# Moving sets of exps from ScalarE to VectorE in three of four head groups, and spreading the adjacency pieces over eight groups

## The chip, the cores and the metric

The kernel runs on one core of a Trainium2 chip. The metric is the time of one execution on the device in microseconds (us). The core has five engines that run side by side, each working through its own instructions in order: TensorE (PE, matrix multiplication into the accumulator memory PSUM), ScalarE (ACT, exponentials and other functions), VectorE (DVE, elementwise work and reductions), GpSimd (POOL) and SyncE (SP), which here only issues DMA transfers. GpSimd issues transfers too. PSUM has eight banks of 512 float32 values in each of its 128 partitions.

## The reference

Four graph layers are applied one after the other to x (3327 tokens, 128 features), each inside a residual sum and a layer normalisation. Almost all the time goes to the first one, an attention in which each of the 128 features acts as a head and the heads' vectors have eight elements:

```python
scale = d ** (-0.5)
q = (x @ Wq.T).reshape(d, n, h)          # d = 128, n = 3327, h = 8
k = (x @ Wk.T).reshape(d, n, h)
v = (x @ Wv.T).reshape(d, n, h)
a = jnp.einsum('dnh,dmh->dnm', q, k) * scale
a = a + spatial_encoding + edge_encoding   # both are adj
a = jax.nn.softmax(a, axis=2)
out = jnp.einsum('dnm,dmh->dnh', a, v)
return out.reshape(n, h * d) @ Wo.T
```

So 128 x 3327 x 3327 exponentials are computed in float32. The other three layers multiply the adjacency matrix (3327 x 3327), normalised by its row or column sums, with x times small weights.

## The kernel before, in words

A first stage computes q, k and v and writes them to memory. Then `attention` runs. It cuts the queries into seven ranges of 476 columns (`CW`) and the keys into 26 tiles of 128, in four key ranges of 7, 7, 6 and 6 tiles (`KBS`). A pair of query range and key range is a block; there are 28, in order of query range and then key range, so that two blocks of seven tiles alternate with two of six. In each block the 128 heads are walked through one by one. Four heads make a group, so a block has 32 groups and the attention has 896. The running number of a group is called n.

**Scores.** The scores of one block stay in seven PSUM banks, `sc`, one per key tile. At a block's first head the transposed adjacency values are written there (L596). After that each head adds only its difference: the operands `kt` and `qt` hold the present head's k and q and, negated, those of the head before (the matmul of L603). Each float32 operand is split into a rounded high part and a low part, which is why 64 rows are contracted. The seven banks are used as three sets, `SETS`: three, two and two tiles in a block of seven, two, two and two in a block of six. Each set has a single buffer. The next head's matmul on a set must wait until the exp of the set is through.

**Exps.** `exponents` takes the sets one after the other, and ScalarE turns each into the numbers `e` with one instruction (L611). In groups whose running number is even, one set, the last of the group's first head, goes to VectorE instead (`vector_exp`, L561 to L574): nine instructions that clamp and scale (L567), round to an integer (L568), take the fraction (L569), build the power of two with a shift (L570), and evaluate a polynomial (L573, five times). L567 reads the scores and so frees the set; the other eight work in SBUF on the single buffers `ey` and `et`.

**Weighing.** `weigh` multiplies the exps of one key tile with the values of the four heads of a group (L628, four matmuls side by side in groups of 32 columns, each with two passes) into the last PSUM bank, `o`. It does so one group later, and three groups accumulate in `o` before VectorE adds it to `acc` (`flush`, L639 and L641). `PLACES` says after which of the twelve sets of the present group each tile of the group before is weighed.

**Order of the work.** All compute engines follow the order in which the instructions are written, and the loop at the end of `attention` writes them. VectorE's steps are kept in a list, `vec`, and let out by two counters in `clock`: one counts the time of the sets, the other the assumed cost of VectorE's steps (`vector_work`). Steps are let out at once where the order demands it: query copies at the start of the next group, an exp before its tiles are weighed. `copy_queries` (L493 to L495) negates and doubles the query rows of the next group after they have arrived. `load_heads` issues the transfers of q and k two groups ahead, `load_values` those of v one group ahead, with a copy on GpSimd (L509).

**Adjacency pieces.** The later layers need the transposed adjacency matrix, its row sums and its column sums. While the attention runs, 91 pieces of 512 x 256 are handled, one in each eight groups (`PACE`). A piece is loaded at n % 8 = 0, transposed and searched for its maximum at 3 (L199, L204), summed by rows and by columns at 5 (L206, L213), and stored by GpSimd at 6 (L234).

Of the kernel before, what the change touches and what calls it, by code (L numbers as in the profile page):

```python
# [20 lines left out]
GROUP = 4  # L21
# [3 lines left out]
PACE = 8  # L25
# [25 lines left out]
def kernel(ctx: ExitStack, tc: tile.TileContext, x, adj, wq, wk, wv, wo,  # L51
# [27 lines left out]
    NHG = D // GROUP  # L79
    KBS = [(0, 7), (7, 7), (14, 6), (20, 6)]  # L80
    assert KBS[-1][0] + KBS[-1][1] == T

    def tokens(t):
        return P - 1 if t == T - 1 else P
# [9 lines left out]
    def flat_ap(dram, at, pattern):  # L94

        f = dram.rearrange("r c -> (r c)")
        if isinstance(at, int):
            base = f[at:at + 1]
        else:
            base = f[ds(at, 1)]  # L100
        return bass.AP(base.tensor, base.offset, pattern)
# [115 lines left out]
    def store_tops(pool, u, top, n):  # L217

        hi = pool.tile([P, 4], F32R, name="rhi")
        nc.vector.tensor_copy(hi, top)  # L220
        lo = pool.tile([P, 4], F32R, name="rlo")
        nc.vector.tensor_tensor(lo, top, hi.bitcast(F32), ALU.subtract)
        for row, sb in enumerate((hi, lo)):
            for i in range(P // n):
                nc.gpsimd.dma_start(out=flat_ap(lead_s[u], row * SUPER + i * P, [[1, n], [n, 4]]),
                                    in_=sb[n * i:n * i + n, :].bitcast(F32))

    def piece_store(pool, u, c, at):
        ns = PIECE // P
        for i in range(4):  # L230
            t = 4 * u + i
            if t < T:
                for q in range(4):
                    nc.gpsimd.dma_start(  # L234
                        out=flat_ap(adjT_s, (t * P + 32 * q) * NP + c * PIECE, [[NP, 32], [P, ns], [1, P]]),
                        in_=at[32 * i:32 * i + 32].rearrange("a (s q) t b -> a q s (t b)", q=4)[:, q])
        if c == NPC - 1:
            nc.vector.tensor_reduce(rsum[:, u, :], sums[u], AX.X, ALU.add)
            if u:
                top = pool.tile([P, 4], F32, name="rtop")  # L240
                nc.vector.tensor_reduce(top, maxima[u], AX.X, ALU.max)
                store_tops(pool, u, top, 32)


    with tc.tile_pool(name="pw", bufs=1) as pw, tc.tile_pool(name="pa", bufs=2) as pa, \
# [110 lines left out]
        d = 0  # L356
# [52 lines left out]
    def attention():  # L409
        with tc.tile_pool(name="acc", bufs=1) as accp, tc.tile_pool(name="kq", bufs=3) as kq, \  # L410
# [14 lines left out]
            blocks = [(min(c, N - CW), kb) for c in range(0, N, CW) for kb in range(len(KBS))]  # L425
            groups = [(b, g) for b in range(len(blocks)) for g in range(NHG)]
            steps = [(b, d) for b in range(len(blocks)) for d in range(D)]

            def load_edges(b):
# [4 lines left out]
                if w < nt * P:  # L434
# [8 lines left out]

            SETS = {7: [(0, 3), (3, 2), (5, 2)], 6: [(0, 2), (2, 2), (4, 2)]}


            PLACES = {7: ((0, 2, 4, 4, 7, 7, 9), (0, 0, 4, 7, 7, 9, 10)),
                      6: ((0, 2, 4, 5, 7, 9), (0, 0, 3, 6, 8, 10))}

            def load_heads(b, g):  # L450

# [45 lines left out]
            def tile_at(nt, i):  # L497

                return (i % 2, i // 2, (i // 2) + ((nt + 1) // 2 if i % 2 else 0))
# [18 lines left out]
            loaded, worked, turning = [], [], []  # L518

            def background(n):  # L520
                if n % PACE == 0 and pieces:
                    u, c = pieces.pop(0)
                    loaded.append((u, c, piece_load(pe, u, c)))
                if n % PACE == 6 and worked:
                    piece_store(pe, *worked.pop(0))

            def background_work(n):
                if n % PACE == 3 and loaded:
                    u, c, ai = loaded.pop(0)
                    steps = piece_work(pe, u, c, ai)  # L530
                    worked.append((u, c, next(steps)))
                    next(steps)
                    clock[1] += 2.4
                    turning.append(steps)
                if n % PACE == 5 and turning:
                    clock[1] += 2.4
                    for _ in turning.pop():
                        pass

            def prepare(b, d):  # L540

                n = b * NHG + d // GROUP
                if d % GROUP == 0:
                    while any(of is None for _, of, _ in vec):
                        vec.pop(0)[2]()
                    if n + 2 < len(groups):
                        heads[groups[n + 2]] = load_heads(*groups[n + 2])
                    if n + 1 < len(groups):
                        values[groups[n + 1]] = load_values(*groups[n + 1])
                    while stores:  # L550
                        store(*stores.pop(0))
                    background(n)

                if d % GROUP == n % 2 and n + 1 < len(groups):
                    vec.extend(copy_queries(*groups[n + 1]))
                if d % GROUP == 3:
                    background_work(n)
# [29 lines left out]
            def exponents(b, d, si):  # L587
                kb = blocks[b][1]
                nt = KBS[kb][1]
                t0, n = SETS[nt][si]  # L590
                s = sc[si]
                if d == 0:
                    for i in range(n):
                        tl = tile_at(nt, t0 + i)[2]
                        for j, (q0, w) in enumerate(subs):
                            nc.tensor.matmul(s[:, i, q0:q0 + w], lhsT=edges[b][0:w, j, tl * P:(tl + 1) * P],  # L596
                                             rhs=ident[0:w, 0:w], is_transpose=True,
                                             start=(j == 0), stop=True, skip_group_check=True)
                kt, qt = heads[b, d // GROUP]
                k = d % GROUP  # L600
                for i in range(n):
                    rg, pos, _ = tile_at(nt, t0 + i)
                    nc.tensor.matmul(s[:, i, 0:CW], lhsT=kt[64 * rg:64 * rg + 64, k, pos * P:(pos + 1) * P],  # L603
                                     rhs=qt[64 * rg:64 * rg + 64, k, :],
                                     start=False, stop=True, skip_group_check=True)
                e = ex.tile([P, (3, 2, 2)[si], CW], F32, tag=f"e{si}", name=f"e{si}", bufs=(6, 7, 8)[si])
                if (b * NHG + d // GROUP) % 2 == 0 and (d % GROUP, si) == (0, 2):
                    vector_exp(e[:, 0:n, :], s[:, 0:n, 0:CW], (b, d // GROUP))
                    clock[1] += 1.2
                else:  # L610
                    nc.scalar.activation(e[:, 0:n, :], s[:, 0:n, 0:CW], AF.Exp, scale=2.0)  # L611
                for i in range(n):
                    es[b, d, t0 + i] = e[:, i, :]
                if d == 0 and si == len(SETS[nt]) - 1 and b + 1 < len(blocks):
                    edges[b + 1] = load_edges(b + 1)
# [38 lines left out]
            queue, place = [], 0  # L654
            with tc.manual_schedule(engines={mybir.EngineType.PE, mybir.EngineType.Activation,
                                             mybir.EngineType.Pool, mybir.EngineType.DVE}):
                edges[0] = load_edges(0)
                for n in range(2):
                    heads[groups[n]] = load_heads(*groups[n])
                for _, _, step in copy_queries(*groups[0]):  # L660
                    step()
                values[groups[0]] = load_values(*groups[0])
                for b, d in steps:
                    prepare(b, d)
                    for si in range(len(SETS[KBS[blocks[b][1]][1]])):
                        vector_work(b)
                        exponents(b, d, si)
                        for _ in range(PLACES[len(queue_of)][d // GROUP % 2 == 0].count(place) if queue else 0):
                            weigh(*queue.pop(0))
                        place += 1  # L670
                    if d % GROUP == GROUP - 1:
                        while queue:
                            weigh(*queue.pop(0))
                        queue_of = [(b, d // GROUP, r) for r in range(KBS[blocks[b][1]][1])]
                        queue, place = list(queue_of), 0
                while queue:
                    weigh(*queue.pop(0))
                while stores:
                    store(*stores.pop(0))
# [283 lines left out]


    attention()
    wide = nc.values_load(flag[0:1, 0:1], min_val=0, max_val=1)
    with tc.If(wide > 0):
# [162 lines left out]
    with tc.manual_schedule(engines={mybir.EngineType.PE, mybir.EngineType.SP}):  # L1130
# [18 lines left out]
        for t in range(T):  # L1149
            n = tokens(t)  # L1150
# [15 lines left out]
        for t in range(T):  # L1166
            n = tokens(t)
# [15 lines left out]
        for t in range(T):  # L1183
            n = tokens(t)
# [16 lines left out]
        for t in range(T):  # L1201
            n = tokens(t)
# [35 lines left out]
```

## Time and profile before

| | us |
|---|---|
| median of 3 runs | 10949.95 |
| lowest and highest run | 10942.28, 10952.19 |
| profiled execution, its own time | 10954.31 |
| profiled execution, first to last instruction (span) | 10952.1 |
| busy: TensorE matmul, ScalarE, VectorE | 10557.4, 9867.2, 7291.7 |
| exps on ScalarE, two tiles: 8512 at | 0.999 |
| exps on ScalarE, three tiles: 1792 at | 1.390 |
| first step of exps on VectorE, two tiles: 448 at | 1.150 |

The profile shows one execution. "Busy" is the time in which an engine has at least one instruction under way. Neighbouring instructions overlap on TensorE and on ScalarE, so that the mean of one times their number is more than the busy time. In group rows a bar separates the number of instructions, the busy time and the mean, and after a second bar comes the idle time of the engine ahead of these instructions with what ended it. A tile name such as `sc` or `e` stands for all of its buffers.

### The profile page before, as it was taken

To read this page: it belongs to the slowest core of one execution; us is meant where nothing else is said; L and a number is where in the kernel's file an instruction comes from. 1 tells how busy PE (TensorE), PEld (TensorE's weight loads), DVE (VectorE), ACT (ScalarE), POOL (GpSimd) and SP (SyncE) were. 2 spreads that over 40 slices of the span, in tenths; PEclk is the share of its full clock that TensorE was granted. 3 is DMA by queue.
4 is the path that set the end of the run, shared out by engine and by line. 5 is a ranking of instruction groups with operands and counts; after the bars stand their busy time and mean duration, and the time that the engine had idled before them with its cause. 6 is when DMAs were issued, how large, how long until landed. Compare 5 with 4: busy or idle time off the path is not lost. (4 is left out here: it accounts for less than half of the span.)

```text
span 10952.1 us, 201583 instructions
## 1 busy us (share of the span) xinstructions
PE 10557.4 (96%) x76941; PEld 4117.7 (38%) x76941; DVE 7291.7 (67%) x8351; ACT 9867.2 (90%) x10783; POOL 1585.4 (14%) x2742
## 2 busy tenths in 40 slices
PE   8899999999999999999999999999999999999999
PEld 5333333333333333333333333333333333333779
DVE  6566776667776677766777667776677766667412
ACT  3799999999999999999999999999999999999400
POOL 0111122111221111211112111121111100001200
PEclk9899999999999999999999999999999999999999
DMA  7988888888888888888888888888888888888676
GB/s 251 155 127 122 128 133 132 127 123 129 134 132 128 123 127 132 135 123 127 128 132 134 120 122 120 123 132 125 127 127 123 120 119 116 115 112 117 207 284 244
DMA packets 995053, 1516.11 MB, mean 138 GB/s; under 512 B 202471, under 2 KB 812577, under 8 KB 980267
## 3 DMA queue, kind: packets, MB, share of 16 engines
q1 hardware_dynamic: 896854, 1371.75, 78.7%
q0 software_dynamic: 79616, 116.88, 4.6%
q8 instruction: 623, 10.21, 0.5%
q10 hardware_dynamic: 17620, 14.49, 0.4%
q14 instruction: 340, 2.79, 0.1%
HBM read 1371.86 MB, written 130.35 MB: 137 GB/s over the span
## 5 line engine op out<-in xcount | busy, mean ns | idle before, releaser
L611 ACT ACTIVATE e<-sc 128x952 f32<-128x952 f32 (+1 forms) x10304 | 9644.5, 1067 | 227.8 <-PE sc L603 219.9
L628 PE MATMUL o<-e,v_pad 128*32 128x476 f32 (+1 forms) x46592 | 5639.9, 573 | 39.9 <-DVE acc L641 36.7
L603 PE MATMUL sc<-qt,kt 64*128 64x476 f32 x23296 | 4474.9, 438 | 252.6 <-ACT e L611 167.3
L603 PEld LDWEIGHTS sc<-qt,kt 64*128 64x128 f32 x23296 | 2187.6, 184 | 4561.8 <-ACT e L611 4254.8
L628 PEld LDWEIGHTS o<-e,v_pad 128*32 128x32 f32 (+1 forms) x46592 | 1039.9, 108 | 1942.4 <-issue 1898.4
L509 POOL COPY v_pad<-vs 128x192 f32<-128x192 f32 (+1 forms) x896 | 441.6, 519 | 8127.9 <-DMA vs<-v_img 6389.5
L567 DVE TENSOR_SCALAR ey<-sc 128x952 f32<-128x952 f32 x448 | 515.0, 1150 | 1631.8 <-PE sc L603 1631.2
L573 DVE SCALAR_TENSOR_TENSOR e<-e,ey 128x952 f32<-128x952 f32 x1344 | 1546.0, 1150 | 43.2
L493 DVE TENSOR_SCALAR qt<-qt 32x1428 fp32r<-32x1428 f32 x896 | 801.8, 895 | 428.9 <-DMA qt<-q_s 347.7
L495 DVE CAST qt<-qt 64x1904 fp32r<-64x1904 f32 x896 | 1035.1, 1155 | 30.5
L234 POOL DMA_DIRECT2D adjT_s<-at x1352 | 796.2, 596 | 185.4 <-DMA adjT_s<-at 130.8
L569 DVE SCALAR_TENSOR_TENSOR ey<-et,ey 128x952 f32<-128x952 f32 x448 | 516.5, 1153 | 15.5
L573 DVE SCALAR_TENSOR_TENSOR e<-e,et 128x952 f32<-128x952 f32 x448 | 514.7, 1149 | 12.5
L573 DVE SCALAR_TENSOR_TENSOR e<-ey 128x952 f32<-128x952 f32 x448 | 515.2, 1150 | 0.0
L1074 PE MATMUL bank<-y,eT 128*128 128x128 f32 (+1 forms) x4056 | 473.9, 276 | 0.4 <-DVE h L1196 0.4
L1074 PEld LDWEIGHTS bank<-y,eT 128*128 128x128 f32 (+1 forms) x4056 | 465.3, 192 | 5.7 <-DVE h L1196 0.6
L641 DVE TENSOR_TENSOR acc<-o,acc 128x476 f32<-128x476 f32 x231 | 150.2, 650 | 422.6 <-PE o L628 422.0
L494 DVE TENSOR_SCALAR qt<-qt 32x476 fp32r<-32x476 f32 x896 | 357.0, 398 | 7.6 <-DMA qt<-lead_s 5.9
L568 DVE TENSOR_SCALAR et<-ey 128x952 f32<-128x952 f32 x448 | 296.9, 663 | 15.4
L570 DVE TENSOR_SCALAR et<-et 128x952 int32<-128x952 int32 x448 | 295.0, 659 | 15.4
L1034 ACT ACTIVATE rstd<-mv,eps 128x1 f32<-128x1 f32 x104 | 30.4, 292 | 265.1 <-DVE mv L1032 265.1
L648 POOL DMA_DIRECT2D o_s<-acc x308 | 191.5, 626 | 35.8 <-DVE acc L641 22.4
(152 smaller groups left out, 2404.6 us busy)
## 6 DMA issues: line engine op xcount, KB each, us to landing
kt<-k_s SPq DMA_DIRECT2D x5320, 96.0 KB
kt<-k_s SPq DMA_DIRECT2D x1764, 128.0 KB
eT<-adjT_s SPq DMA_DIRECT2D x78, 1664.0 KB
qt<-q_s SPq DMA_DIRECT2D x896, 119.0 KB
qt<-q_s SPq DMA_DIRECT2D x1792, 59.5 KB
vs<-v_img SPq DMA_DIRECT2D x224, 224.0 KB
adjT_s<-at POOLq DMA_DIRECT2D x1352, 32.0 KB, 5.2
vs<-v_img SPq DMA_DIRECT2D x224, 192.0 KB
```

Of the source, the lines that this page charges most:

```text
L234: nc.gpsimd.dma_start(out=flat_ap(adjT_s, (t * P + 32 * q) * NP + c * PIECE, [[NP, 32], [P, ns], [1, P]]), in_=at[32 * i:32 * i + 32].rear ...
L493: return [(0.9, None, lambda: nc.vector.tensor_scalar(qt[32:64, 1:], qf[0:32, 0:GROUP - 1], -1.0, None, ALU.mult)), (0.4, None, lambda: nc ...
L494: (0.4, None, lambda: nc.vector.tensor_scalar(qt[32:64, 0], before, -1.0, None, ALU.mult)),
L495: (1.2, None, lambda: nc.vector.tensor_copy(qt[64:128], qf[0:64]))]
L509: nc.gpsimd.tensor_copy(vp[:, 32:32 + nt * GROUP * 32].rearrange("p (x c) -> p x c", c=32)[:, :, 0:H], vs.rearrange("p (x c) -> p x c", c=H))
L567: nc.vector.tensor_scalar(y, x, -58 * math.log(2.0), 2 / math.log(2.0), ALU.max, ALU.mult)
L569: vec.append((1.2, of, lambda: nc.vector.scalar_tensor_tensor(y, t, ROUND, y, ALU.subtract, ALU.subtract)))
L573: vec.append((1.2, of, lambda i=i, a=a: nc.vector.scalar_tensor_tensor(e, e if i else y, a, t if i == len(POLY) - 1 else y, ALU.add, ALU.m ...
L603: nc.tensor.matmul(s[:, i, 0:CW], lhsT=kt[64 * rg:64 * rg + 64, k, pos * P:(pos + 1) * P], rhs=qt[64 * rg:64 * rg + 64, k, :], start=False ...
L611: nc.scalar.activation(e[:, 0:n, :], s[:, 0:n, 0:CW], AF.Exp, scale=2.0)
L628: nc.tensor.matmul(o[32 * j:32 * j + 32, 0:CW], lhsT=values[b, g][:m, c:c + 32], rhs=es[b, g * GROUP + j, r][:m, :], start=(r == 0 and u = ...
L1074: nc.tensor.matmul(ps[:n, 0:D], lhsT=e[:m, s, :n], rhs=y[:m, s, col:col + D], start=(s == 0), stop=(s == T - 1))
```

## The change

In blocks of seven tiles VectorE takes its set of exps in the first three of four groups rather than in every second group; in blocks of six it stays with every second one. `PLACES` gets one list for each of four groups. The lists of six tiles are the same for the same group as before; those of seven are new for three of the four. The query copies are put in the list `vec` at the first head of a group with a vector exp and at the second head of one without. Of the adjacency pieces, the sums move from n % 8 = 5 to 7 and the store from 6 to 0 of the next eight, ahead of the next piece's load in the written order.

```diff
             SETS = {7: [(0, 3), (3, 2), (5, 2)], 6: [(0, 2), (2, 2), (4, 2)]}
 
-
-            PLACES = {7: ((0, 2, 4, 4, 7, 7, 9), (0, 0, 4, 7, 7, 9, 10)),
-                      6: ((0, 2, 4, 5, 7, 9), (0, 0, 3, 6, 8, 10))}
+            def on_vector(nt, g):
+
+                return g % 4 != 3 if nt == 7 else g % 2 == 0
+
+
+
+            PLACES = {7: ((0, 0, 4, 7, 7, 10, 10), (0, 0, 4, 7, 7, 9, 10), (1, 1, 4, 6, 8, 10, 10),
+                          (0, 2, 3, 5, 7, 8, 10)),
+                      6: ((0, 0, 3, 6, 8, 10), (0, 2, 4, 5, 7, 9)) * 2}
...
             def background(n):
+                if n % PACE == 0 and worked:
+                    piece_store(pe, *worked.pop(0))
                 if n % PACE == 0 and pieces:
                     u, c = pieces.pop(0)
                     loaded.append((u, c, piece_load(pe, u, c)))
-                if n % PACE == 6 and worked:
-                    piece_store(pe, *worked.pop(0))
...
-                if n % PACE == 5 and turning:
+                if n % PACE == 7 and turning:
                     clock[1] += 2.4
...
-                if d % GROUP == n % 2 and n + 1 < len(groups):
+
+                if d % GROUP == 1 - on_vector(KBS[blocks[b][1]][1], d // GROUP) and n + 1 < len(groups):
                     vec.extend(copy_queries(*groups[n + 1]))
...
-                if (b * NHG + d // GROUP) % 2 == 0 and (d % GROUP, si) == (0, 2):
+                if on_vector(nt, d // GROUP) and (d % GROUP, si) == (0, 2):
                     vector_exp(e[:, 0:n, :], s[:, 0:n, 0:CW], (b, d // GROUP))
...
-                        for _ in range(PLACES[len(queue_of)][d // GROUP % 2 == 0].count(place) if queue else 0):
+                        for _ in range(PLACES[len(queue_of)][d // GROUP % 4].count(place) if queue else 0):
                             weigh(*queue.pop(0))
```

## The prediction

> **What bounds the kernel now.** I began with the page's busy times.
>
> ```profile
> PE 10557.4 (96%) x76941; PEld 4117.7 (38%) x76941; DVE 7291.7 (67%) x8351; ACT 9867.2 (90%) x10783; POOL 1585.4 (14%) x2742
> PE   8899999999999999999999999999999999999999
> ACT  3799999999999999999999999999999999999400
> ```
>
> TensorE (PE) and ScalarE (ACT) are both nearly full, VectorE (DVE) a third idle. By the trace's first and last exps attention runs from 334 to 10181 us. Next, groups of instructions with shapes kept apart (busy us, mean ns, then idle time before):
>
> ```profile
> L611 ACT ACTIVATE e<-sc 128x952 f32<-128x952 f32 x8512 | 7615.3, 999 | 180.3 <-PE sc L603 172.5
> L611 ACT ACTIVATE e<-sc 128x1428 f32<-128x1428 f32 x1792 | 2490.4, 1390 | 47.5 <-PE sc L603 47.5
> L567 DVE TENSOR_SCALAR ey<-sc 128x952 f32<-128x952 f32 x448 | 515.0, 1150 | 1631.8 <-PE sc L603 1631.2
> ```
>
> The exps leave ACT 228 us idle; 448 sets are on DVE. Then a busy table for four successive groups of heads of a seven-tile block, each from its first score matmul to the next group's (vector, none, vector, none):
>
> ```profile
> core 0: us, PE busy (x) PEld busy (x) DVE busy (x) ACT busy (x) POOL busy (x), PEclk, DMA share, GB/s
> 2216.45:2228.07 11.62, 11.37 (x84) 4.12 (x86) 8.20 (x9) 11.62 (x12) 0.69 (x2) 1.00 1.01 145
> 2228.07:2239.45 11.38, 10.93 (x87) 3.76 (x83) 4.42 (x6) 11.38 (x13) 0.00 (x0) 1.00 0.88 123
> 2239.45:2251.07 11.62, 11.38 (x84) 4.12 (x86) 10.29 (x12) 11.62 (x12) 1.67 (x2) 1.00 0.75 102
> 2251.07:2262.45 11.38, 10.93 (x87) 3.75 (x83) 8.11 (x9) 11.38 (x13) 0.00 (x0) 1.00 0.92 118
> ```
>
> The group with one exp fewer on ACT is longer by TensorE's starts. By ACT's starts, which I averaged from single records, it is shorter: 11.23 us against 11.80. So TensorE loses 0.41 us of its lead over ACT in a vector group and regains it in the other. That decides the case. Last, the timeline of the first group (start, us, rows merged):
>
> ```profile
> 2216.45 0.70 PE L603 MATMUL sc<-qt,kt 64*128 64x476 f32 x3 [0.49 <-ACT e L611]
> 2217.07 1.80 PE L628 MATMUL o<-e,v_pad 128*32 128x476 f32 x16
> 2218.81 1.30 PE L603 MATMUL sc<-qt,kt 64*128 64x476 f32 x7
> 2219.63 1.15 DVE L567 TENSOR_SCALAR ey<-sc 128x952 f32<-128x952 f32 x1 [6.59 <-PE sc L603]
> 2220.36 0.49 PE L603 MATMUL sc<-qt,kt 64*128 64x476 f32 x2 [0.25 <-ACT e L611]
> ...
> 2227.99 1.15 DVE L573 SCALAR_TENSOR_TENSOR e<-e,et 128x952 f32<-128x952 f32 x1
> ```
>
> Two tiles of weighing (x16) stand between the first set of scores and the second; TensorE is late there and ACT waits for it. One vector exp takes 2219.63 to 2229.14, 9.51 us.
>
> **What the Trainium skill says.** "ScalarE: Activation LUTs", What ACT_TABLE_LOAD costs: an ACTIVATE with immediates takes 186 ns + 0.833 ns per element, 979 and 1376 ns here; the trace has 999 and 1390. It gives 93 ns of overlap between neighbours; the trace more, 0.84 us start to start after a two-tile set and 1.24 after a three-tile one, which I use. "VectorE: DVE Perf Modes", The perf-mode tier table: one-source fp32 from SBUF runs at 2×, reads from PSUM and two-tensor operations at 1×; the trace agrees, 663 ns for L568, 1150 for L567 and L573. "TensorEngine Tiling (Array Packing)", Key Properties: a change of tiling mode drains TensorE. Scores use 64 rows, weighing 32 columns, and single records show 0.49 us from the last pass of weighing to a score matmul, 0.41 between passes.
>
> **The change part by part.**
>
> *Removed.* Fourteen of the 28 blocks have seven tiles; vector groups go from 16 to 24 of 32 in each, so 112 sets leave ACT. At 0.84 us that is 94 us of ACT, but the saving is what TensorE lets through. From single records (medians, 98 vector groups): a two-tile exp starts 0.53 us after its scores start, a three-tile one 0.79; scores may overwrite a set 0.06 after its exp ends; exps last 0.97 and 1.40; two score matmuls run side by side in 0.32; weighing a tile takes 0.83, 0.92 if scores follow. With these I walk the new order through four groups A, B, C (vector) and D, each timed from its first score matmul; (d,i) is set i of head d.
>
> A is the old vector group with tile 5 weighed one place later. Scores of (3,1) start at 9.00, when exp (2,1) has freed the bank; weighing 9.42 and 10.24; scores (3,2) 11.17; B starts at 11.49 (now 11.64). The next exp starts at 12.55, 1.06 into B, where A's started at 1.47.
>
> B: scores (0,1) wait behind two tiles weighed, 2.28; their exp starts at 2.81, 1.75 after the first one instead of 1.24. Then as in A: exp (1,0) 3.70, (2,0) 6.63, (3,0) 9.56, scores (3,2) 11.24; C at 11.56.
>
> C: the two tiles come one place later; scores (0,2) 2.56, (1,0) 2.88, exp (1,0) 3.67, where ACT could have started at 3.13. Exp (2,1) 7.83, scores (3,1) 8.89, tiles 5 and 6 at 9.31, scores (3,2) 11.06; D at 11.38.
>
> D is bound by ACT: its exps enter at 1.05, twelve take 11.68 plus 0.11 where scores come late (exp (3,0)), leaving at 1.46 of the next A, so 11.38.
>
> Sum 45.81, against 2 × (11.637 + 11.377) = 46.03 now. So 0.22 a round; 0.33 if the 0.11 in D is not lost. Taking 0.28, times 112 rounds: **31 us saved**; ends 0.05 and 0.57 (ACT's own difference between the two kinds of group), 6 and 64 us.
>
> *Added on DVE.* 112 × 9.51 = 1065 us. A round is 3 × 9.51 + 4 × 2.4 (query copies, L493 to L495) + 0.9 (flushes) + 2.4 (half a piece) = 41.4 of 45.8 us, 90%, so it fits on average. Behind the waiting L567 stands everything else of DVE, and TensorE waits for its two banks. A's exp runs 3.18 to 12.69, 1.2 into B; three copies stand ahead of B's L567, which starts at 3.65 and ends at 4.8. TensorE wants the banks at 5.18: 0.35 to spare. B's exp ends 1.6 into C; one copy (0.9) is ahead, so L567 waits for its scores at 3.04. C's ends with its late copies 2.8 into D; D has no exp and takes its copies and piece half by 7.6. Each result is weighed at place 8 or later, after 7 us: no wait. The cover of 0.35 is gone where A has a flush: L641 ends about 0.69 into B, TensorE's first weighing, due at 0.55, waits, and L567 slips by 0.65. A third of rounds, 37, at about 0.2 each: **7 us lost**, ends 0 and 16.
>
> *Moved.* Piece sums go from the sixth to the eighth group of eight, which has no exp in either kind of block; DVE idles there, nothing is paid. The same instructions are issued. Piece stores (about fifteen POOL DMAs of 32 KB, some 9 us of issue at 596 ns) go from the seventh group to the first, beside the piece load, where the DMA share is already 1.01. "DMA: Bandwidth & Descriptors", Issuing engines are not separate DMA queues, says that all issuers share the same sixteen engines; no row here shows both in one group. POOL's value copy stands ahead of the store in that group, and the next one's result is wanted two groups later. The store's buffer is wanted three groups on, at 5.2 us to landing: covered. Late next are query rows: at starts of blocks L493 already waits (347.7 us in 154 waits), and by single records the third group is 1.3 to 5.5 us too long for it in most blocks that begin new query columns. The store may make them 2 us later; against that L567 now goes ahead of two copies there. Zero, ends −10 and +12.
>
> *Six-tile blocks.* PLACES is rewritten to the same lists for the same groups, and exps are unchanged: nothing.
>
> Sum: 10952.1 − 31 + 7 = 10928 for the profiled span; the median of the runs is 2 lower, so **10926 us**.
>
> **Rivals.** *TensorE is no bound*: the extra waits at the start of B and C dissolve, because TensorE used lead it will rebuild. For it: only 1.4 us of score waits on ACT show in those four groups, and TensorE's own work there is about 11 us a group. Against: the lead is lost in each vector group. 0.57 × 112 = 64 saved: 10886.
>
> *Nothing measurable*: 0.05 to 0.2 a round, the walk's own error. 10940.
>
> *Slower, through L567 in B and C*: if DVE reaches it 0.35 later than worked out (a copy waiting for query rows, gaps of 0.03 that add up), the banks come late. Past that point each microsecond late is paid by TensorE, and DVE at 90% cannot catch up before D. At 0.35 paid in both groups: 78 − 31 = 47 lost: 10997. Against it: no DVE work is left over when a round ends.
>
> That the sets don't move is no rival: the built order has 560 of L567's kind and each follows the preceding exp's last step.
>
> **How the numbers follow.** Forecast 0.42, TensorE no bound 0.15, nothing measurable 0.28, slower 0.15. No change is what stays within 0.2%, 22 us, about what a measurement of this kernel can tell. So faster 0.42 + 0.15 = 0.57, same 0.28, slower 0.15. The range goes from the second case's 10886 to 10962, which leaves out most of the slow case. The forecast's own range is 10906 to 10928.
>
> **What would show it.** ACT exps 10192, L567's kind 560, DVE busy near 8340. Groups near 11.5, 11.55, 11.4, 11.4. If C and B are 11.2, the walk was too strict; if they exceed 11.7 with scores released by DVE, L567 is late. If the third groups of blocks grow beyond 3 us, it is the stores. The forecast is wrong if ACT's intervals after (0,0) are not about 1.75 in B.

## The result, and the profile after

The changed kernel takes 10915.21 us (median of 8 runs, 10909.79 to 10919.46) against 10947.38 for the kernel before on the same occasions (8 runs, 10939.01 to 10953.98): a ratio of 0.9971, 95% interval 0.9962 to 0.9979, 32 us less. 10926 was forecast. The profiled execution's span fell from 10952.1 to 10913.7 us, 38.4 less.

Lines have moved in the changed kernel: the score matmul is L610 (before L603), ScalarE's exp L618 (L611), the reading of scores on VectorE, the first step of its exp, L574 (L567), weighing L635 (L628), the query copies L499 to L501 (L493 to L495), the flush L646 and L648 (L639 and L641). The page after, busy times, and the slices of PE and ACT:

```profile
PE 10590.0 (97%) x76941; PEld 4114.5 (38%) x76941; DVE 8351.7 (77%) x9359; ACT 9774.0 (90%) x10671; POOL 1667.9 (15%) x2742
PE   8899999999999999999999999999999999999999
ACT  3799999999999999999999999999999999999400
```

ACT is busy 93 us less (112 sets at 0.84 are 94), DVE 1060 us more (112 exps at 9.51 are 1065). Only about a third of what left ACT shows up in the time. The groups of instructions that answer to those of before (busy us, mean ns, idle time before and what ended it):

```profile
L618 ACT ACTIVATE e<-sc 128x952 f32<-128x952 f32 x8400 | 7532.5, 1006 | 209.5 <-PE sc L610 203.2
L618 ACT ACTIVATE e<-sc 128x1428 f32<-128x1428 f32 x1792 | 2518.2, 1405 | 71.6 <-PE sc L610 71.5
L574 DVE TENSOR_SCALAR ey<-sc 128x952 f32<-128x952 f32 x560 | 643.9, 1150 | 1047.2 <-PE sc L610 1041.2
```

ACT's idle time for scores rose from 228 to 281 us: TensorE is more often the later of the two. The busy table of four successive groups A, B, C, D in the same block as in the view of before, each from its first score matmul to the next group's:

```profile
core 0: us, PE busy (x) PEld busy (x) DVE busy (x) ACT busy (x) POOL busy (x), PEclk, DMA share, GB/s
2203.01:2214.47 11.46, 11.21 (x86) 4.23 (x86) 8.09 (x8) 11.46 (x12) 8.34 (x16) 1.00 0.96 158
2214.47:2225.96 11.49, 11.08 (x86) 3.98 (x84) 10.70 (x13) 11.26 (x12) 1.06 (x2) 1.00 1.05 149
2225.96:2237.17 11.21, 11.03 (x86) 3.93 (x84) 10.92 (x12) 10.99 (x12) 1.72 (x2) 1.00 0.78 114
2237.17:2248.68 11.51, 11.51 (x87) 3.54 (x84) 10.60 (x12) 11.51 (x13) 0.00 (x0) 1.00 0.93 117
```

The sum of the round is 45.67 us, against 46.00 in the four rows of before. ACT is no longer busy throughout in B and C, and TensorE shows no gap in D. The POOL time in A is the piece store that moved there. (Busy time alone does not say which engine is the limit: ends of matmuls in the trace are modelled, and exps overlap, so that a short wait between them does not show as idle. The experiments below decide it.) The start of B in the timeline (start, us; rows of equal instructions merged, some left out):

```profile
2214.99 1.80 PE L635 MATMUL o<-e,v_pad 128*32 128x476 f32 x16
2215.71 0.89 DVE L499 TENSOR_SCALAR qt<-qt 32x1428 fp32r<-32x1428 f32 x1
2216.53 0.39 DVE L500 TENSOR_SCALAR qt<-qt 32x476 fp32r<-32x476 f32 x1
2216.72 1.14 PE L610 MATMUL sc<-qt,kt 64*128 64x476 f32 x7
2216.95 1.15 DVE L501 CAST qt<-qt 64x1904 fp32r<-64x1904 f32 x1
2217.25 3.94 ACT L618 ACTIVATE e<-sc 128x952 f32<-128x952 f32 x4 [0.23 <-PE sc L610]
2218.13 1.15 DVE L574 TENSOR_SCALAR ey<-sc 128x952 f32<-128x952 f32 x1
2218.27 0.48 PE L610 MATMUL sc<-qt,kt 64*128 64x476 f32 x2 [0.41 <-ACT e L618]
```

ACT waits 0.23 us for scores that stand behind two tiles of weighing, TensorE then 0.41 for the exp of them, and DVE reads its set after three copies, 3.66 us into the group. This is what the walk had: by medians over the groups B of the table below, the exp after the first one starts 1.69 us later, where the forecast named 1.75 as its sign.

Medians of the group lengths, from single records of the fifth to thirty-first groups of all seven-tile blocks (98 each of A, B and C, 84 of D), for all kernels of this study whose rounds differ. Before, A and C are the groups with a vector exp, B and D those without.

| kernel | A | B | C | D | round |
|---|---|---|---|---|---|
| before | 11.64 | 11.37 | 11.64 | 11.38 | 46.02 |
| changed | 11.46 | 11.52 | 11.20 | 11.51 | 45.69 |
| one place changed, no exp moved | 11.47 | 11.51 | 11.47 | 11.51 | 45.95 |
| exps moved, old lists | 11.63 | 11.52 | 11.52 | 11.38 | 46.05 |
| changed, a set less in D | 11.46 | 11.52 | 11.20 | 11.50 | 45.68 |
| changed, ACT relieved throughout | 11.28 | 11.52 | 10.88 | 11.44 | 45.12 |
| changed, reading in B 1.15 us late | 11.46 | 12.32 | 11.23 | 11.51 | 46.53 |
| changed, C's list in A and B, old list in D | 11.72 | 11.37 | 11.36 | 11.51 | 45.96 |

### The profile page after: what moved, and what is told of

Read it like the earlier page. It is cut to its first block, busy times and chain, and to the rows that moved or that the text cites. A ratio compares the mean times of both kernels' runs of the same rounds, so it can differ in the third digit from the quotient of the medians.

```text
span 10913.7 us, 202710 instructions
## 1 busy us (share of the span) xinstructions
PE 10590.0 (97%) x76941; PEld 4114.5 (38%) x76941; DVE 8351.7 (77%) x9359; ACT 9774.0 (90%) x10671; POOL 1667.9 (15%) x2742
## 5 line engine op out<-in xcount | busy, mean ns | idle before, releaser
L618 ACT ACTIVATE e<-sc 128x952 f32<-128x952 f32 (+1 forms) x10192 | 9551.3, 1076 | 281.1 <-PE sc L610 274.7
L635 PE MATMUL o<-e,v_pad 128*32 128x476 f32 (+1 forms) x46592 | 5657.5, 573 | 47.1 <-DVE acc L648 39.8
L610 PE MATMUL sc<-qt,kt 64*128 64x476 f32 x23296 | 4503.2, 439 | 178.4 <-ACT e L618 113.1
L610 PEld LDWEIGHTS sc<-qt,kt 64*128 64x128 f32 x23296 | 2197.0, 184 | 4570.9 <-ACT e L618 4015.0
L580 DVE SCALAR_TENSOR_TENSOR e<-e,ey 128x952 f32<-128x952 f32 x1680 | 1932.7, 1150 | 52.3
L515 POOL COPY v_pad<-vs 128x192 f32<-128x192 f32 (+1 forms) x896 | 534.4, 622 | 7986.1 <-DMA vs<-v_img 5559.1
L635 PEld LDWEIGHTS o<-e,v_pad 128*32 128x32 f32 (+1 forms) x46592 | 1027.9, 108 | 1904.7 <-issue 1858.7
L574 DVE TENSOR_SCALAR ey<-sc 128x952 f32<-128x952 f32 x560 | 643.9, 1150 | 1047.2 <-PE sc L610 1041.2
L501 DVE CAST qt<-qt 64x1904 fp32r<-64x1904 f32 x896 | 1032.8, 1153 | 30.4
L499 DVE TENSOR_SCALAR qt<-qt 32x1428 fp32r<-32x1428 f32 x896 | 807.6, 901 | 159.2 <-DMA qt<-q_s 100.6
L580 DVE SCALAR_TENSOR_TENSOR e<-e,et 128x952 f32<-128x952 f32 x560 | 647.5, 1156 | 17.8
L576 DVE SCALAR_TENSOR_TENSOR ey<-et,ey 128x952 f32<-128x952 f32 x560 | 645.1, 1152 | 19.4
L580 DVE SCALAR_TENSOR_TENSOR e<-ey 128x952 f32<-128x952 f32 x560 | 642.0, 1146 | 0.0
L648 DVE TENSOR_TENSOR acc<-o,acc 128x476 f32<-128x476 f32 x231 | 150.3, 651 | 312.4 <-PE o L635 312.0
L575 DVE TENSOR_SCALAR et<-ey 128x952 f32<-128x952 f32 x560 | 372.6, 665 | 18.7
L577 DVE TENSOR_SCALAR et<-et 128x952 int32<-128x952 int32 x560 | 371.1, 663 | 19.3
```

Of the source, the lines that this page charges most:

```text
L499: return [(0.9, None, lambda: nc.vector.tensor_scalar(qt[32:64, 1:], qf[0:32, 0:GROUP - 1], -1.0, None, ALU.mult)), (0.4, None, lambda: nc ...
L501: (1.2, None, lambda: nc.vector.tensor_copy(qt[64:128], qf[0:64]))]
L515: nc.gpsimd.tensor_copy(vp[:, 32:32 + nt * GROUP * 32].rearrange("p (x c) -> p x c", c=32)[:, :, 0:H], vs.rearrange("p (x c) -> p x c", c=H))
L574: nc.vector.tensor_scalar(y, x, -58 * math.log(2.0), 2 / math.log(2.0), ALU.max, ALU.mult)
L575: vec.append((0.7, of, lambda: nc.vector.tensor_scalar(t, y, ROUND, None, ALU.add)))
L576: vec.append((1.2, of, lambda: nc.vector.scalar_tensor_tensor(y, t, ROUND, y, ALU.subtract, ALU.subtract)))
```

## The experiments

Every time stands beside runs of the kernel before on the same chip; ratios are to those, with 95% intervals. The changed kernel's own ratio is 0.9971 (0.9962 to 0.9979).

### Which of the two parts

The exps without the moved pieces:

```diff
-                if n % PACE == 0 and worked:
-                    piece_store(pe, *worked.pop(0))
                 if n % PACE == 0 and pieces:
                     u, c = pieces.pop(0)
                     loaded.append((u, c, piece_load(pe, u, c)))
+                if n % PACE == 6 and worked:
+                    piece_store(pe, *worked.pop(0))
...
-                if n % PACE == 7 and turning:
+                if n % PACE == 5 and turning:
```

> The change without its second part: exps and lists as changed, piece sums at n % 8 = 5 and stores at 6 as before. Theory (VectorE has 0.35 us to spare in B and less in C, so a piece's half must lie in D): the sums of 2.4 us fall into a group B, once in eight groups, and make the reading of scores in the next C about 1.2 us late. Some 46 such groups lie in blocks of seven tiles: 55 us, so about 10970. Rival one (VectorE is only 90% busy in a round and absorbs it): 10915, as the whole change. Rival two (moving the pieces cost time through the stores): 10905.

Measured: 10912.53 us, ratio 0.9966 (0.9954 to 0.9978). The whole gain is there without the second part. The sums do fall into B, but C after them is only 0.11 us longer (mean of 11.32 against 11.21). My reason was wrong in one point: L574 is written at once, while the other steps wait in the list; with DVE behind, the written order lets L574 of C go ahead of the copies and even of the last step of B's exp:

```profile
1900.11 3.61 DVE L580 SCALAR_TENSOR_TENSOR e<-e,ey 128x952 f32<-128x952 f32 x3
1903.86 1.15 DVE L574 TENSOR_SCALAR ey<-sc 128x952 f32<-128x952 f32 x1
1904.92 1.14 DVE L580 SCALAR_TENSOR_TENSOR e<-e,et 128x952 f32<-128x952 f32 x1
1906.09 0.99 DVE L499 TENSOR_SCALAR qt<-qt 32x1428 fp32r<-32x1428 f32 x1
```

What piles up is work that nobody waits for soon. Rival one came true.

The pieces without the exps, the reverse edit in the kernel before:

```diff
+                if n % PACE == 0 and worked:
+                    piece_store(pe, *worked.pop(0))
                 if n % PACE == 0 and pieces:
                     u, c = pieces.pop(0)
                     loaded.append((u, c, piece_load(pe, u, c)))
-                if n % PACE == 6 and worked:
-                    piece_store(pe, *worked.pop(0))
...
-                if n % PACE == 5 and turning:
+                if n % PACE == 7 and turning:
```

> The second part alone: the kernel before with the piece sums at n % 8 = 7 and the stores at 0. Theory: nothing is paid and nothing won, 10947 within 5. Rival (the wait of L493 for query rows, 348 us before and 101 after, fell because the pieces moved, and the shorter first groups of blocks and the 8 us of the six-tile blocks come from there): 22 less, 10925.

Measured: 10958.4 us, ratio 1.0008 (1.0000 to 1.0016), some 9 us longer, at the edge of what the interval allows. Neither expectation holds. Its profile has one group that the kernel before has not: the eleventh of block 16 is 10.0 us too long. The changed kernel has the same one, 9.9 us too long. The chain can be read there. SyncE's own waits in the changed kernel between 6020 and 6070 us:

```profile
SPq L184 <- POOL ai L176: 14.3, 1, 14.3
SPq L476 <- DMA ai<-in_adj_dram: 8.1, 3, 3.5
```

And GpSimd's timeline there:

```profile
6030.36 4.49 POOL L234 DMA_DIRECT2D adjT_s<-at  x8 [0.26 <-issue]
...
6040.19 2.72 POOL L234 DMA_DIRECT2D adjT_s<-at  x4 [0.43 <-DMA adjT_s<-at]
6042.90 2.98 POOL L225 DMA_DIRECT2D lead_s<-rhi  x4
6045.86 1.10 POOL L225 DMA_DIRECT2D lead_s<-rlo  x2
6047.66 1.09 POOL L225 DMA_DIRECT2D lead_s<-rlo  x2 [0.69 <-issue]
6048.74 0.97 POOL L176 MEMSET ai<- 128x1024 f32 x1
```

This is the first piece of the last, incomplete row range. GpSimd clears its buffer (L176) before SyncE may load it. The clearing now stands behind the store of the piece before, which ends a row range: sixteen transfers and eight more for the maxima, 18.4 us from the start of the first to the end of the last. SyncE holds at the load for 14.3 us, and behind it in its queue are the query and key rows of the coming groups. In the timeline of all engines:

```profile
6062.69 0.89 DVE L499 TENSOR_SCALAR qt<-qt 32x1428 fp32r<-32x1428 f32 x1 [8.34 <-DMA qt<-q_s]
6063.62 1.15 DVE L574 TENSOR_SCALAR ey<-sc 128x952 f32<-128x952 f32 x1
6064.82 1.56 PE L610 MATMUL sc<-qt,kt 64*128 64x476 f32 x5 [8.44 <-DVE ey L574]
```

DVE waits 8.34 us for query rows, L574 stands behind that, and TensorE waits 8.44 us for its banks. Every profile here with the store at n % 8 = 0 has a stall at this group or this and the next, of 5.6 to 10.9 us together; the three profiles with the store at 6 have none there. The moved store thus costs about 10 us, once, in this kernel's order. Keeping the store's old group avoids it, as the first of these two runs did; the gain from that is too small to be told from no gain in the times.

### The moved sets or the lists

One number of the kernel before:

```diff
-            PLACES = {7: ((0, 2, 4, 4, 7, 7, 9), (0, 0, 4, 7, 7, 9, 10)),
+            PLACES = {7: ((0, 2, 4, 4, 7, 7, 9), (0, 0, 4, 7, 7, 10, 10)),
```

> The kernel before with one number changed: in its vector groups of seven-tile blocks tile 5 is weighed at place 10 and not at 9, as in group A of the change; no exp is moved. Theory (TensorE paces, and each group's length goes by its list): the vector group falls from 11.64 to 11.46 us and the next stays at 11.38; 0.17 in 224 pairs, 38 us, about 10909: as much as the whole change gave. Rival (the gain of the change comes from the sets taken off ScalarE): no change, 10947.

Measured: 10938.28 us, ratio 0.9991 (0.9983 to 1.0000): 9 us, with no gain just within the interval. The vector group fell to 11.47 as expected, but the next rose to 11.51. TensorE comes there 0.17 us earlier and finds ScalarE with twelve sets. The busy table shows ScalarE busy for the whole of both groups:

```profile
2212.67:2224.13 11.46, 11.21 (x85) 4.24 (x86) 8.08 (x8) 11.46 (x12) 0.69 (x2) 1.00 1.03 134
2224.13:2235.64 11.51, 11.06 (x87) 3.73 (x83) 4.54 (x7) 11.51 (x13) 0.00 (x0) 1.00 0.99 131
```

The kernel before shows the same, so the starts have to decide: from the first exp of the second group to its twelfth it is 10.96 us (median), and 10.84 with the walk's distances, seven of 0.84 and four of 1.24. ScalarE has almost no wait there.

The moved exps with the old lists:

```diff
-            PLACES = {7: ((0, 0, 4, 7, 7, 10, 10), (0, 0, 4, 7, 7, 9, 10), (1, 1, 4, 6, 8, 10, 10),
-                          (0, 2, 3, 5, 7, 8, 10)),
+            PLACES = {7: ((0, 0, 4, 7, 7, 9, 10), (0, 0, 4, 7, 7, 9, 10), (0, 0, 4, 7, 7, 9, 10),
+                          (0, 2, 4, 4, 7, 7, 9)),
```

> The changed kernel with the lists of before for weighing: the old vector list in A, B and C, the other in D. All exps stay where the change put them. Theory (TensorE paces by list): A 11.64, B 11.52, C about 11.55, D 11.38, sum 46.1, so nothing is left of the gain: about 10950. Rival (moving the sets gives the gain): 10915 to 10925.

Measured: 10949.3 us, ratio 1.0001 (0.9993 to 1.0009). Nothing is left. The sets are off ScalarE, DVE has done them, and TensorE makes nothing of it: a round of 46.05 us, where the expectation had 46.1. Its profile has two more differences, of opposite sign: the stall of the moved store, 9.3 us here, and shorter starts of blocks, the first four groups of seven-tile blocks taking 683 us in sum where the kernel before took 701. So moving sets is worth nothing in a round with the old lists, and one list's number without moved sets is worth some 9 us; neither alone gave 32. What all four lists would give without moved sets was not tried, so that a part of the 32 for them alone is not excluded.

A set less in D, which is computed by no engine (`fixed` is a tile of ones):

```diff
+                if nt == 7 and d // GROUP % 4 == 3 and (d % GROUP, si) == (0, 2):
+                    for i in range(n):
+                        es[b, d, t0 + i] = fixed[:, i, :]
...
+                    return
```

> The changed kernel, where in each group D (the fourth, without a vector exp) the last set of the first head is computed by no engine; the weighing reads constants in its place. ScalarE has eleven sets in every group of a seven-tile block. Theory (TensorE paces a group with eleven sets): D falls from 11.51 us to between 11.2 and 11.45, 6 to 35 us in 112 groups, so 10880 to 10909. Rival (ScalarE paces, and a set taken off it is worth the 0.57 us between the two kinds of group before, or its full 0.84): 64 to 94 us, 10821 to 10851.

Measured: 10912.8 us, ratio 0.9966 (0.9954 to 0.9978); D at 11.50 us. That is below even the low end of the first expectation's gain. D's row of the busy table says why:

```profile
2236.88:2248.37 11.49, 11.49 (x87) 3.53 (x83) 10.61 (x12) 10.99 (x12) 0.00 (x0) 1.00 0.88 123
```

ScalarE now has 0.5 us free, TensorE none. The starts show it without modelled ends: scores (3,0) come 9.29 us into D in this run as in the changed kernel (medians). With the change's list, D is TensorE's own; the last set left on ScalarE in the fourth group is not worth moving.

ScalarE relieved in all groups, by exps of eight columns (`some`) in place of whole ones:

```diff
+                if nt == 7 and si == 2 and (d % GROUP or d // GROUP % 4 == 3):
+                    nc.scalar.activation(some, s[:, 0:n, 0:8], AF.Exp, scale=2.0)
+                    for i in range(n):
+                        es[b, d, t0 + i] = fixed[:, i, :]
...
+                    return
```

> The changed kernel, where in seven-tile blocks the exp of the third set reads only 8 columns of each tile (in every head but those whose set VectorE has), and the weighing reads constants in its place: ScalarE is relieved of three sets more in A, B, C and of four in D, while TensorE has the same instructions and VectorE the same exps. Theory (TensorE's own pace by the walk's intervals is about 11.0 us a group, and 0.2 to 0.5 of the rest is waiting for sets): a round falls from 45.69 to 44.0 to 44.5, 135 to 190 us, 10725 to 10780. Rival one (TensorE has no waits left): 10900 or more. Rival two (ScalarE is the main bound): below 10600.

Measured: 10882.83 us, ratio 0.9937 (0.9921 to 0.9952), 0.0034 below the changed kernel's ratio, which is 37 us. The round is 45.12, between the two expectations and nearer to "no waits left". One round's busy table:

```profile
2191.08:2202.37 11.29, 10.87 (x86) 4.29 (x86) 7.90 (x8) 9.85 (x12) 6.52 (x13) 1.00 0.97 154
2202.37:2213.88 11.51, 11.10 (x88) 3.99 (x85) 11.00 (x13) 9.47 (x12) 3.74 (x5) 1.00 0.97 169
2213.88:2225.11 11.23, 10.78 (x86) 3.93 (x84) 10.93 (x12) 9.24 (x11) 2.23 (x2) 1.00 0.78 105
2225.11:2236.54 11.43, 11.43 (x86) 3.51 (x83) 10.63 (x12) 8.73 (x13) 0.00 (x0) 1.00 0.92 118
```

ScalarE is free for 8 us of the round, and TensorE shortens it by 0.57. So taking this much more work off ScalarE is worth no more than that in these lists. The sets that stay still have their own waits, so this is no bound on what other orders could give. My 44.0 to 44.5 for TensorE's own pace was too low.

### How much VectorE has to spare

The last query copy listed twice for group C:

```diff
-                        (1.2, None, lambda: nc.vector.tensor_copy(qt[64:128], qf[0:64]))]
+                        *[(1.2, None, lambda: nc.vector.tensor_copy(qt[64:128], qf[0:64]))]
+                        * (2 if KBS[blocks[b][1]][1] == 7 and g % 4 == 2 else 1)]
```

> The changed kernel, where in each group B of a seven-tile block the last query copy (1.15 us) is done twice, so that VectorE reads its scores 1.15 us later. Theory (0.35 us to spare): TensorE gets the two banks 0.8 us late in 112 groups, and the copy ahead in C adds nothing: 90 us, about 11005. Rival (the wait is taken from TensorE's other waits and ScalarE's slack, since neither is bound alone): under 20 us, 10915 to 10935.

Measured: 10914.3 us, ratio 0.9969 (0.9958 to 0.9980). The edit missed its aim: the list let the repeat out behind L574 in most groups, and B's reading started at 3.66 us as before. What it does show is that 1.15 us more work in a round of VectorE, behind the reading, cost nothing measurable. The aim was met by writing the copies out ahead of the reading:

```diff
+                    if nt == 7 and d // GROUP % 4 == 1:
+                        while any(of is None for _, of, _ in vec):
+                            vec.pop(0)[2]()
+                        to = heads[b, d // GROUP + 1][1]
+                        for _ in range(1):
+                            nc.vector.tensor_copy(to[64:128], to.bitcast(F32)[0:64])
                     vector_exp(e[:, 0:n, :], s[:, 0:n, 0:CW], (b, d // GROUP))
```

> The changed kernel, where in B the three query copies and a repeat of the last one (1.15 us, same data) are put ahead of the reading of scores, so that it is late by 1.15 us; in the last experiment of this kind the extra copy had been let out behind the reading. Theory (0.35 us to spare): B's scores (1,2) start at about 6.0 instead of 5.15, 0.8 us longer in 112 groups, 90 us, 11005. Rival (absorbed by TensorE's other waits): below 20 us, under 10935.

Measured: 11024.75 us, ratio 1.0073 (1.0058 to 1.0089), slower than before the change. Its timeline in B, where L620 is the repeated copy:

```profile
2241.06 1.15 DVE L620 CAST qt<-qt 64x1904 fp32r<-64x1904 f32 x1
2242.24 1.15 DVE L574 TENSOR_SCALAR ey<-sc 128x952 f32<-128x952 f32 x1
2243.44 1.14 PE L610 MATMUL sc<-qt,kt 64*128 64x476 f32 x7 [0.83 <-DVE ey L574]
```

The median of B rose by 0.80 us, to 12.32, its mean by 0.92, which is 103 us in 112 rounds where the ratios differ by 112. Its 1.20 us delay of the reading (3.67 to 4.87) had 0.4 us of cover, where the prediction had 0.35. The rival that ended on the slower side has its place and price right in B (no run delayed C); the change stays short of it by that margin.

The opposite, the copies behind the reading in B, which by the written order puts them behind it in C as well:

```diff
+                late = KBS[blocks[b][1]][1] == 7 and d // GROUP % 4 == 1
-                if d % GROUP == 1 - on_vector(KBS[blocks[b][1]][1], d // GROUP) and n + 1 < len(groups):
-                    vec.extend(copy_queries(*groups[n + 1]))
+                if d % GROUP == (1 if late else 1 - on_vector(KBS[blocks[b][1]][1], d // GROUP)) and n + 1 < len(groups):
+                    vec[0 if late else len(vec):0 if late else len(vec)] = copy_queries(*groups[n + 1])
```

> The changed kernel, where in B the query copies are let out behind the reading of scores; by the written order they then lie behind it in C as well. Theory (in a third of the rounds a flush in A makes the reading in B late by 0.3 us, and a late query row in C holds it up): 7 to 15 us less, 10900 to 10908. Rival (the reading is on time as it is): 10915.

Measured: 10918.51 us, ratio 0.9972 (0.9962 to 0.9983): nothing gained. The reading in B went from 3.67 to 3.08 us (medians), and B stayed at 11.52, its mean at 11.59. It had been on time.

### Looking for a better version

C's list in A and B, and the old list in D:

```diff
-            PLACES = {7: ((0, 0, 4, 7, 7, 10, 10), (0, 0, 4, 7, 7, 9, 10), (1, 1, 4, 6, 8, 10, 10),
-                          (0, 2, 3, 5, 7, 8, 10)),
+            PLACES = {7: ((1, 1, 4, 6, 8, 10, 10), (1, 1, 4, 6, 8, 10, 10), (1, 1, 4, 6, 8, 10, 10),
+                          (0, 2, 4, 4, 7, 7, 9)),
```

> The changed kernel with C's list in A and B too and the old list of a group without vector exp in D. Theory (length goes by list): A and B fall to 11.20, D to 11.38, sum 44.98 against 45.69: 80 us, 10835. Rival (C is short only because it follows B, or VectorE reads B's scores too late for this list, which wants the banks at 4.68 where the reading ends at 4.82): half or less, 10875 or above.

Measured: 10927.41 us, ratio 0.9981 (0.9973 to 0.9988), 11 us longer than the changed kernel by ratios, so the theory fails and the rival's side holds. A length doesn't go by its own list: A became 11.72, and C, whose list was not touched, 11.36. What a list gives depends on where the groups around it leave TensorE. Why A got longer was not taken apart further.

The old list in D alone, and with the copies behind the reading:

```diff
-                          (0, 2, 3, 5, 7, 8, 10)),
+                          (0, 2, 4, 4, 7, 7, 9)),
```

> The changed kernel with the old list of a group without vector exp in D. Theory (D returns to 11.38): 0.13 in 112 rounds, 15 us, 10900. Rival (what D wins the next A gives back, as the group after the mended one did in the kernel before): 10910 to 10920.

> Both of the last two edits together. If they are independent, the sum of their differences; if D's is given back, as the first of them alone, about 10905.

Measured: 10912.1 us, ratio 0.9963 (0.9950 to 0.9977), and 10913.34, ratio 0.9969 (0.9957 to 0.9981). D stayed at 11.51 in both, for another reason than with the change's list: with the old one its exps run from first to twelfth in 10.96 us (10.84 without waits), so that ScalarE is the limit. Two limits lie at the same length there, and changing the list alone passes from one to the other. None of the versions here is faster than the changed kernel by more than the intervals allow.

## Why the prediction was right, and where it was not

**TensorE lets only part of it through.** Right. The lead that TensorE loses in a vector group was the reading that decided, and the walk through A to D gave 45.81 us where the medians have 45.69: A 11.49 (measured 11.46), B 11.56 (11.52), C 11.38 (11.20), D 11.38 (11.51). A, B and the 1.69 us are the mechanism as forecast; C and D are not. In C I let the exp of (1,0) start 0.79 us after its scores; these run straight behind others there, and it starts at 0.69 (2.80 to 3.49), which moves ScalarE's chain through the group up. In D the new list puts the weighing into seven separate places; scores (3,0) came at 9.29, my intervals had 9.13. "D is bound by ACT" was the wrong limit with this list: with a set less on ScalarE these scores come at the same time and D stays at 11.50. That the two errors, 0.18 too much in C and 0.13 too little in D, nearly cancel is luck.

**The sum.** By means over all these groups but the one stalled C, a round went from 46.08 to 45.80 us, 0.28; 112 rounds are 32 us. Forecast were 31 less 7. That 32 is also the measured difference is partly luck: the stall takes 10 of them back, which leaves 22. In the profiled pair, which differs by 38.4, the other 16 lie mostly in the first four groups of blocks: beyond these rounds' share, 10 in blocks of seven tiles and 6 in blocks of six. The forecast put both the moved pieces and the starts of blocks at zero.

**The rivals.** "TensorE is no bound" is refuted: the set less in D, worth nothing, and the relieved ScalarE, worth 37 us for 8 us a round, show it. "Nothing measurable" is what the sets do with the old lists. My 31 us stood under "removed", as a saving of sets; the runs put them under the change's sets and lists together.

**The flush, 7 us lost.** The size holds, and half of the step. B's mean is 0.08 above its median, 9 us in 112. In the 28 groups B of the table that follow a flush in A, the flush ends 0.65 into B and TensorE's first weighing starts at 0.79; in the other 70 it starts at 0.52. B is 11.78 us long in the ones and 11.52 in the others. So the late weighing is right. That L567 slips by 0.65 is wrong: L574 starts at 3.36 after a flush and at 3.72 otherwise, and with the reading 0.6 us earlier the difference in length is the same.

**0.35 us to spare for L574 in B.** Right: L574 started at 3.67 (forecast 3.65), and a delay of 1.20 us was paid for by 0.80.

**Moved pieces, zero.** Wrong, by about 10 us, within its ends of −10 and +12 but through another step. I listed the value copy ahead of the store on GpSimd and looked for trouble in shared DMA engines. I missed the instruction behind the store on that queue, the clearing of L176, and that SyncE's load waits for it with the rows of coming groups behind. It is a moved step whose price lies in the queue it was moved into.

**Block starts, neutral.** Not settled. L499's wait for query rows fell from 348 to 101 us, and the third groups of seven-tile blocks were 10 us too long in sum instead of 22. But the same sum is between 0 and 21 in the profiles with moved exps, so a gain can't be put to it alone. A gain at the starts as a whole is likely: the first four groups of seven-tile blocks take 697 to 701 us in sum in the three profiles without moved exps and 677 to 697 in the eleven with them, where shorter rounds explain about 4 us. Which step gives it was not taken apart.

## What to carry to other kernels

When two engines are nearly full and coupled by single buffers, work taken off one of them may show only if the other's order is rearranged at the same time, as here; time each of its steps by single records before counting the saving. Count a moved step at what stands behind it in its new queue, rare instructions such as the clearing for a ragged last piece too. An engine that is nearly 90% busy, as VectorE is in these rounds (40.3 of 45.7 us), may cost nothing so long as the one step that others wait for can overtake its backlog.

## What was not expected of the hardware

I had taken 0.32 us for two score matmuls side by side. Single records show two speeds. A pair that follows directly on another lasts 0.38 us, and the next starts 0.22 us after it (medians); the first pair after weighing or after a wait for a bank lasts 0.48, and the next starts 0.32 us after it. The ends are modelled in the trace, the starts are not, and the starts alone give the difference. In C of the block shown the scores (0,2), behind weighing, start at 2.49 and last 0.48, those of (1,0) at 2.81 and 3.03 last 0.38; in A the same scores (1,0) had waited for their bank and last 0.48. So each break costs about 0.1 us beyond the wait itself, besides the 0.09 that the prediction counted at the end of weighing. This fits TensorE taking 11.20 us for the same instructions in one order and 11.51 in another; that it is the whole of the difference was not shown.
